# Layer 2's expert rows go to sorted places by indirect scatters instead of being fetched by inverted indices, and layer 1's experts run in a fixed VectorE order

## The chip, the cores and the metric

The kernel runs on one core of a Trainium2 chip, as one program in one launch. The metric is the device time of that program in microseconds (us), from its first instruction to its last, as a median of several runs. The engines are called as in the profile: PE is TensorE (matmuls and transposes), DVE is VectorE, ACT is ScalarE, POOL is GpSimd, and SP is SyncE, which issues DMA transfers. POOL issues the indirect DMAs, in which a column of indices says which row of a DRAM table each of 128 partitions reads or writes. A tile is 128 rows (tokens) of 128 floats.

## The reference: what is computed

The input is 2 x 1024 tokens of 128 numbers. Four layers follow each other, each of the form half an FFN, attention, half an FFN, all on a residual stream x:

```
for layer in 0, 1, 2:
    x = x + 0.5 * ffn(layernorm(x));  x = x + attn(layernorm(x));  x = x + 0.5 * ffn(layernorm(x))
layer 3:  the same, with a recurrence in the place of attention
```

Two of the FFNs matter here.

Layer 1's FFN picks, for every token and each of 8 blocks j, one of 64 hidden units by an argmax, and uses that unit alone:

```
lr   = x @ m1                                   # 128 -> 64
quant_mask = argmax(lr @ m2 + mb, axis=-1)      # per token: 8 choices out of 64
mid  = relu(x @ w1)[j, quant_mask[j]]           # of 512 hidden units, 8 stay
out  = mid @ w2[j, quant_mask[j]] + b2
```

Layer 2's FFN is a mixture of 8 experts, of which each token uses two:

```
gate_vals, gate_idx = top_k(x @ router_w, 2);  gates = softmax(gate_vals)
h   = gelu(x @ w1[e] + b1[e])                   # 128 -> 512
res = x + h @ w2[e] + b2[e]
y   = sum over the two experts of gates * (normed(res) * gamma[e] + beta[e])
```

## The kernel before

**Tokens and order of work.** x stays in SBUF as 16 tiles of 128 tokens, in four quarters of four tiles. The order of PE's instructions is the order in which the program is written (`manual_schedule(engines={PE})`); instructions of the other engines are ordered by a list scheduler at build time, which goes by its own cost model, unless `keep_in_program_order` holds them in the written order. Side work is woven into PE's order by a virtual clock: `later` starts a thread of small pieces with pauses between them, `tick(us)` moves the clock on and lets the threads whose pause is over do their next piece, and `need` finishes a thread at once. PSUM is split into three kinds of buffers, two of each: `pair` (two banks), `long` and `bank` (one bank each).

**Layer 1's FFN** (`l1_ffn`, L700 to L774) runs twice: once ahead of layer 1's attention (914 to 1012 us of the profile) and once after it (1482 to 1590 us), where the norms, the router and the routes of layer 2 are woven in by ticks. For every tile t there are these steps:

- `choose`: two matmuls into the two banks of one pair, the mask logits (L717) and the hidden units (L718); DVE takes the maximum of every block, mx (L722), and marks where it is, eq (L723); POOL multiplies eq by descending numbers, so that the first of equal maxima is largest (L724); ACT takes the relu of the hidden units, av (L726).
- `first`: DVE takes the maximum of the multiplied marks, fi (L732), and POOL subtracts it (L733), so that the chosen unit stands at zero.
- `chosen`: DVE multiplies av by "eq is zero" (L736).
- `output`: PE transposes av (L741), ACT copies it to aT (L743). `add`: PE multiplies by w2 (L748, L750), DVE adds the product to x (L751).

In iteration t stand first(t-1), chosen(t-2), choose(t), output(t-4) and add(t-5), with ticks of 5.0 us of virtual time in all.

**Layer 2's experts.** The tokens are taken in two halves of 1024, twice: e1 is the FFN ahead of layer 2's attention, e2 the one after it. A half goes through these steps:

- `l2_ffn_prep` normalizes two quarters, stores the normalized rows to a DRAM table xd (L1253, by SP) and computes router and gates.
- `l2_route` finds for every (token, choice) pair its place in a list sorted by expert, in which each expert's rows start at a new tile: counts by PE (L1290 to L1296), then small DVE operations that end in r_si, the 16 columns of places (L1321), and r_exi, the expert of each tile (L1326). At most 23 tiles can be in use. Then the places are inverted: DVE makes one-hot matrices (L1330 to L1342), PE multiplies them (L1347, 16 matmuls), and DVE turns the product into r_tok (L1354, L1355), which says for every place which token stands there.
- `L2Experts` works on the 23 tiles in groups of four. `gather` (L1396) fetches each tile's rows from xd by r_tok, with one indirect DMA on POOL per tile. `fetch` (L1409) loads the tile's expert weights, w1b and b2g, with SP. `ahead` keeps two or three groups of rows and six tiles of weights ahead. Then PE transposes the rows (L1442), computes the hidden layer (L1454) and the output (L1470), and DVE and SP normalize and store the result to a DRAM table yd.
- `l2_back` (L1539) fetches every token's two results from yd by r_si, with indirect DMAs on POOL, and adds them to x.

Of the kernel before, what the change touches and what calls it, by code (L numbers as in the profile page):

```python
# [19 lines left out]
P = 128  # L20
# [161 lines left out]

def norm_pieces(c, r, q, scale=1.0, eps=1e-5, weight=None, by=2, wait=(4.5, 4.0)):


    def xs(j):
        return c.x[:, 4 * q + j, :]

    def apply():
        r["xn"] = c.act.tile([P, 4, P], F32, tag="xn", name="xn", bufs=2)  # L190
        norm_apply(c, r, xs, r["xn"], 0, by)

    def turn():
        r["xT"] = by_feature(c, q if by == 2 else 0, r["xn"], weight)

    return [partial(norm_stats, c, r, xs, (scale, eps)), wait[0], apply, wait[1], turn, 2.0]
# [503 lines left out]
def l1_ffn(c, w, rs, key, done, ticks=1):  # L700
    nc = c.nc
    with c.pool("l1f", 2) as pool:
# [11 lines left out]
        def choose(t):  # L714
            s_ = slice(t % 4 * P, (t % 4 + 1) * P)
            pr = c.pair("pr")
            nc.tensor.matmul(pr[:, 0, :], lhsT=rs[t // 4]["lr"][:, s_], rhs=w["m2mb"], start=True, stop=True)  # L717
            nc.tensor.matmul(pr[:, 1, :], lhsT=rs[t // 4]["xT"][:, s_], rhs=w["w1"], start=True, stop=True)  # L718
            pm = pr[:, 0, :].rearrange("p (j y) -> p j y", j=8)
            mx = pool.tile([P, 8], F32, tag="mx", name="mx")  # L720
            eq = pool.tile([P, 8, 64], F32, tag="eq", name="eq", bufs=4)
            nc.vector.tensor_reduce(mx, pm, AX.X, ALU.max)  # L722
            nc.vector.tensor_tensor(eq, pm, mx.unsqueeze(2).to_broadcast([P, 8, 64]), ALU.is_equal)  # L723
            nc.gpsimd.tensor_mul(eq, eq, w["rev"].unsqueeze(1).to_broadcast([P, 8, 64]))  # L724
            av = pool.tile([P, 512], F32, tag="av", name="av", bufs=5)
            nc.scalar.activation(av, pr[:, 1, :], AF.Relu)  # L726
            return eq, av

        def first(eq, av):

            fi = pool.tile([P, 8], F32, tag="fi", name="fi")
            nc.vector.tensor_reduce(fi, eq, AX.X, ALU.max)  # L732
            nc.gpsimd.tensor_sub(eq, eq, fi.unsqueeze(2).to_broadcast([P, 8, 64]))  # L733

        def chosen(eq, av):
            nc.vector.scalar_tensor_tensor(av, eq.rearrange("p j y -> p (j y)"), 0.0, av, ALU.is_equal, ALU.mult)  # L736

# [18 lines left out]
        av, aT = {}, {}  # L756
        for t in range(NT + 5):
            if 0 <= t - 1 < NT:
                first(*av[t - 1])
            if 0 <= t - 2 < NT:  # L760
                chosen(*av[t - 2])
            if t < NT:
                av[t] = choose(t)
                if t % 4 == 2 and t // 4 < 3:
                    latent(t // 4 + 1)
            if ticks > 1:
                c.tick(5.0 / ticks)
            if 0 <= t - 4 < NT:
                aT[t - 4] = output(t - 4, av.pop(t - 4)[1])
            if ticks > 2:  # L770
                c.tick(5.0 / ticks)
            if 0 <= t - 5 < NT:
                add(t - 5, aT.pop(t - 5))
            c.tick(5.0 / ticks)  # L774

# [409 lines left out]
def l2_consts(c, pool):  # L1185
    w = {n: c.load(pool, f"l2f_{n}") for n in "router beta".split()}

    nc = c.nc
    shapes = dict(iota=[P], lower=[8, 8], pidx=[1], tcol=[2, 8])
    w |= {n: pool.tile([P] + shape, F32, tag=n, name=n) for n, shape in shapes.items()}  # L1190
    w["before"] = pool.tile([P, P], BF16, tag="before", name="before")
    nc.vector.tensor_scalar(w["before"], c.causal, -1.0, None, ALU.is_lt)
    pi = c.bank("pi")
    nc.tensor.matmul(pi[:, 0:P], lhsT=c.ones16, rhs=w["before"], start=True, stop=True)
    nc.tensor.matmul(pi[:, P : P + 1], lhsT=w["before"], rhs=c.ones16[:, 0:1], start=True, stop=True)
    nc.vector.tensor_copy(w["iota"], pi[:, 0:P])
    nc.vector.tensor_copy(w["pidx"], pi[:, P : P + 1])
    for k in range(2):
        nc.vector.tensor_copy(w["tcol"][:, k, :], pi[:, 0:8])
    eight = w["iota"][:, 0:8]  # L1200
    nc.vector.tensor_tensor(
        w["lower"],
        eight.unsqueeze(2).to_broadcast([P, 8, 8]),
        eight.unsqueeze(1).to_broadcast([P, 8, 8]),
        ALU.is_gt,
    )
    return w
# [22 lines left out]


def l2_half(c, dpool, name, qs):


    h = {"name": name, "qs": qs, "ready": 0, "then": []}
    h["xd"] = dpool.tile([S, P], F32, tag=f"xd{name}", name="xd")
    h["yd"] = dpool.tile([TILES * P, P + 1], F32, tag=f"yd{name}", name="yd")
    return h


def l2_ffn_prep(c, w, keep, h, a):
    nc = c.nc
    q, r = h["qs"][a], {}
    tiles = slice(4 * a, 4 * a + 4)
    norm = norm_pieces(c, r, q, by=8)

# [4 lines left out]

    def store():
        nc.sync.dma_start(out=h["xd"][512 * a : 512 * a + 512, :].rearrange("(j p) d -> p j d", p=P), in_=r["xn"])  # L1253

    def chosen():
        h["ready"] += 1
        if h["ready"] == 2:
            c.later(("route", h["name"]), l2_route(c, w, keep, h) + h["then"])
# [4 lines left out]
    )  # L1263
    return [begin] + norm[:3] + [store] + norm[3:] + gates[:1] + [chosen] + gates[1:]


def l2_route(c, w, keep, h):
# [59 lines left out]

    def one_hot():
        hi, hif, lo = tile_([16], "hi", I32), tile_([16], "hif"), tile_([16], "lo")
        nc.vector.tensor_scalar(hi, h["si"], 7, None, ALU.logical_shift_right)  # L1330
        nc.vector.tensor_copy(hif, hi)
        nc.vector.scalar_tensor_tensor(lo, hif, -float(P), r["sl"], ALU.mult, ALU.add)
        b = tile_([16, 24], "b")
        r["b"] = tile_([16, 2, 24], "b16", BF16)
        nc.vector.tensor_tensor(b, wide(w["iota"][:, 0:24], 16), long(hif, 24), ALU.is_equal)
        nc.vector.tensor_scalar(r["b"][:, :, 0, :], b, w["pidx"], None, ALU.mult)
        nc.vector.tensor_tensor(r["b"][:, :, 1, :], b, long(w["tcol"].rearrange("p k t -> p (k t)"), 24), ALU.mult)
        r["lo"] = lo

    def one_hot_row():  # L1340
        r["a"] = tile_([16, P], "a", BF16)
        nc.vector.tensor_tensor(r["a"], wide(w["iota"], 16), long(r["lo"], P), ALU.is_equal)  # L1342

    def invert():
        pt = r["pt"] = c.bank("pt")[:, 0:48]
        for k in range(16):
            nc.tensor.matmul(  # L1347
                pt, lhsT=r["a"][:, k, :], rhs=r["b"][:, k].rearrange("p a i -> p (a i)"), start=(k == 0), stop=(k == 15)
            )

    def tokens():
        h["tok"] = keep.tile([P, 24], I32, tag="r_tok", name="r_tok", bufs=2)
        low = tile_([24], "low")
        nc.vector.tensor_copy(low, r["pt"][:, 0:24])  # L1354
        nc.vector.scalar_tensor_tensor(h["tok"], r["pt"][:, 24:48], float(P), low, ALU.mult, ALU.add)  # L1355

    return [pairs, 2.0, count, 1.0, places, one_hot, one_hot_row, 9.0, invert, 1.0, tokens, 0.1]


class L2Experts:  # L1360
# [12 lines left out]
    def routed(self, n):  # L1373

        h = self.groups[n][0]
        return "tok" in h

# [11 lines left out]
    def gather(self):  # L1389
# [3 lines left out]
        self.xg[n] = self.keep.tile([P, 4, P], F32, tag="xg", name="xg", bufs=4)  # L1393
        for j, i in enumerate(g):
            at = bass.IndirectOffsetOnAxis(ap=h["tok"][:, i : i + 1], axis=0)
            self.nc.gpsimd.indirect_dma_start(self.xg[n][:, j, :], None, h["xd"], at)  # L1396
        self.gathered += 1
# [20 lines left out]
    def ahead(self, k):  # L1418

        h = self.groups[self.tiles[k][0]][0]  # L1420
        if "tok" not in h:
            for a in range(2):
                self.c.need(("half", h["qs"][a]))
            self.c.need(("route", h["name"]))

        some = 2 if any(self.c.waits(("back", h["name"])) for h in self.halves) else 3
        while self.gathered < min(self.tiles[k][0] + some, len(self.groups)) and self.routed(self.gathered):
            self.gather()
# [612 lines left out]
def macaron(ctx: ExitStack, tc: tile.TileContext, dram: dict, out: bass.AP):  # L2041
# [36 lines left out]
    with ExitStack() as s1:  # L2078
        with tc.tile_pool(name="w0", bufs=1) as p0:
            w = l0_weights(c, p0)  # L2080
            sets = l2_sets(c, dpool)
            r = [chunks() for _ in range(8)]
            for q in range(NC):
# [20 lines left out]
        wa = l2_attn_weights(c, s2.enter_context(c.pool("w2a")))  # L2104
        def halves(n, parts):

            hs = [l2_half(c, dpool, f"{n}{k}", qs) for k, qs in enumerate(parts)]

# [3 lines left out]

            return hs, prep

        h1, prep1 = halves(1, ((0, 1), (2, 3)))
        h2, prep2 = halves(2, ((0, 2), (1, 3)))
        s4 = ctx.enter_context(ExitStack())
# [145 lines left out]
```

## Time and profile before

| | |
|---|---|
| median of 7 runs | 2940.45 us (2939.42 to 2948.44) |
| the profiled execution's own time | 2940.06 us |
| its span, first to last instruction | 2938.3 us, so 1.76 us lie outside the span |
| mean granted TensorE clock | 0.952 of full speed |
| busiest engine | PE, 89% of the span |

The table of the profile's instructions names engine, line and operation, as in "DVE L732 ... fi<-eq": VectorE, line 732, writes fi from eq. In the timeline a row gives start, length, and, in brackets, how long the engine had stood idle before it and which instruction on which engine ended that. The lengths of neighbours can overlap a little, as an instruction's start is logged before its predecessor's end. A row "x4" stands for four instructions of one kind in a run. The windows give busy time per engine in a stretch of the span:

| window (us) | PE busy | DVE busy | ACT busy | POOL busy | granted clock |
|---|---|---|---|---|---|
| 920 to 960 | 34.82 | 32.64 | 12.18 | 22.30 | 0.91 |
| 960 to 1000 | 30.59 | 35.32 | 14.83 | 22.25 | 0.87 |
| 1520 to 1540 | 10.74 | 14.73 | 5.06 | 6.93 | 0.75 |
| 1540 to 1560 | 15.89 | 18.21 | 5.40 | 8.23 | 0.91 |
| 1560 to 1580 | 12.77 | 12.73 | 4.71 | 3.35 | 0.68 |
| 1580 to 1600 | 13.73 | 11.78 | 6.31 | 10.84 | 0.84 |

Indirect DMAs on POOL take 0.95 us of its time each and follow each other every 1.25 us. There are 92 of them for xg (`gather`; the median from issue to landing is 3.4 us) and 64 for yg (`l2_back`; 3.1 us).

### The profile page before, as it was taken

How to read it: one execution, taken by the hardware profiler on the slowest of the kernel's cores; microseconds unless marked ns; L12 is line 12 of the kernel's file. 1: busy time of each engine (PE TensorE's matmuls, PEld its weight loads, DVE VectorE, ACT ScalarE, POOL GpSimd, SP SyncE). 2: the span in 40 equal slices, each digit the busy share in tenths (PEclk: the TensorE clock that was granted, in tenths of full speed). 3: DMA queues.
4: the chain of work that ended last, by engine and by line, in shares of the span. 5: the costliest groups of instructions: out<-in, count | busy, mean ns of one | idle time of the engine just before them, and what ended most of it. 6: DMA issues, size and time to landing. Idle time of an engine off the chain costs nothing. (4 is left out here: it accounts for less than half of the span.)

```text
span 2938.3 us, 42431 instructions
## 1 busy us (share of the span) xinstructions
PE 2606.5 (89%) x14226; PEld 1492.1 (51%) x14226; DVE 2061.0 (70%) x6460; ACT 1597.2 (54%) x3188; POOL 1011.9 (34%) x941
## 2 busy tenths in 40 slices
PE   8899999899999779988977859999989999879999
PEld 5544445444465555444446843333433433776667
DVE  5566667666656888869666667777876776668874
ACT  3355555455533456666623517667766777444543
POOL 0133322223203554445433444334443443442110
PEclk9899999999999878999998979999999999889999
DMA  4000000000000000000002820000000011650000
GB/s 126 8 15 15 15 15 8 15 15 8 8 22 1 1 1 1 1 1 1 30 33 84 227 60 2 1 1 1 1 1 8 1 38 43 174 157 22 1 5 11
DMA packets 69768, 86.52 MB, mean 29 GB/s; under 512 B 14334, under 2 KB 49935, under 8 KB 68912
## 3 DMA queue, kind: packets, MB, share of 16 engines
q1 hardware_dynamic: 60816, 71.71, 8.7%
q0 software_dynamic: 4992, 10.27, 1.7%
q8 instruction: 114, 1.87, 0.3%
q10 hardware_dynamic: 3744, 1.84, 0.2%
q14 instruction: 102, 0.84, 0.1%
HBM read 66.18 MB, written 12.38 MB: 27 GB/s over the span
## 5 line engine op out<-in xcount | busy, mean ns | idle before, releaser
L1694 ACT ACTIVATE pe<-ps 128x1024 f32<-128x1024 f32 x256 | 249.1, 1021 | 205.5 <-PE ps L1687 205.5
L518 ACT ACTIVATE pe<-ps,nm 128x512 f32<-128x512 f32 (+3 forms) x384 | 219.8, 578 | 144.6 <-DVE nm L516 121.6
L1687 PE MATMUL ps<-tr 64*128 64x512 f32 x1024 | 262.6, 632 | 0.0
L1720 PE MATMUL po<-pe,v 128*64 128x512 f32 x1024 | 250.9, 611 | 1.0 <-ACT pe L1695 1.0
L1695 ACT ACTIVATE pe<-pe 128x2048 f32<-128x2048 f32 x128 | 244.6, 1911 | 4.0
L516 DVE TENSOR_REDUCE nm<-ps 128x2 f32<-128x256 f32 (+1 forms) x192 | 183.1, 954 | 60.8 <-PE ps L505 56.8
L348 DVE SCALAR_TENSOR_TENSOR x<-py,gates,x 128x128 f32<-128x128 f32 x448 | 133.1, 343 | 130.4 <-PE py L311 130.4
L505 PE MATMUL ps<-kT,qT 64*128 64x512 f32 (+3 forms) x768 | 179.4, 545 | 16.2 <-ACT pe L518 9.2
L533 PE MATMUL ptp<-ident,pe 128*128 128x128 f32 x1152 | 172.6, 284 | 16.0 <-ACT pT L104 9.4
L533 PEld LDWEIGHTS ptp<-ident,pe 128*128 128x128 f32 x1152 | 123.8, 141 | 116.5 <-issue 56.2
L547 PE MATMUL po<-pT,v 128*64 128x512 f32 (+3 forms) x768 | 166.7, 513 | 0.0
L1463 ACT ACTIVATE hT<-ph,w1b 128x128 f32<-128x128 f32 x368 | 105.4, 368 | 98.9 <-issue 62.2
L1707 POOL TENSOR_TENSOR acp<-pe 128x1024 f32<-128x1024 f32 x32 | 78.3, 2446 | 219.9 <-ACT pe L1695 196.5
L1720 PEld LDWEIGHTS po<-pe,v 128*64 128x64 f32 x1024 | 62.8, 138 | 174.5 <-issue 159.7
L104 ACT COPY pT<-ptp 128x512 f32<-128x512 f32 x192 | 91.9, 478 | 108.3 <-PE ptp L533 107.5
L1072 POOL TENSOR_SCALAR pe<-pe,rs 128x256 f32<-128x256 f32 (+7 forms) x128 | 95.2, 757 | 139.8 <-DVE rs L1069 56.6
L1687 PEld LDWEIGHTS ps<-tr 64*128 64x128 f32 x1024 | 90.4, 190 | 103.9 <-issue 72.6
L311 PEld LDWEIGHTS py<-l3f_w,hT 128*128 128x128 f32 x1024 | 126.8, 197 | 23.4 <-issue 19.1
L1610 POOL TENSOR_TENSOR sq<-raw 128x512 f32<-128x512 f32 x64 | 88.6, 1385 | 138.1 <-DVE raw L1608 104.0
L468 POOL TENSOR_TENSOR kT<-tab 128x512 f32<-128x512 f32 x32 | 40.6, 1268 | 266.8 <-DVE tab L467 135.7
L311 PE MATMUL py<-l3f_w,hT 128*128 128x128 f32 x1024 | 128.8, 281 | 2.5 <-ACT hT L300 2.5
L1454 PE MATMUL ph<-xgT,w1b 128*128 128x128 f32 x736 | 109.8, 297 | 21.8 <-ACT hT L1463 11.6
(418 smaller groups left out, 6264.4 us busy)
## 6 DMA issues: line engine op xcount, KB each, us to landing
w1b<-sets SPq DMA_DIRECT2D x92, 258.0 KB
b2g<-sets SPq DMA_DIRECT2D x92, 128.0 KB
two<-two SPq DMA_DIRECT2D x64, 128.0 KB
yd<-y SPq DMA_DIRECT2D x20, 258.0 KB
l2f_w<-in_l2f_w SPq DMA_DIRECT2D x2, 2048.0 KB
sets<-in_l2f_w SPq DMA_DIRECT2D x1, 2048.0 KB
xd<-xn SPq DMA_DIRECT2D x8, 256.0 KB
l3f_w<-in_l3f_w SPq DMA_DIRECT2D x2, 1024.0 KB
```

Source lines behind the costliest of these rows:

```text
L311: nc.tensor.matmul(py[:, j, :], lhsT=hT[:, k, j * P : (j + 1) * P], rhs=w2[:, e, k, :], start=(k == 0), stop=(k == hc - 1),)
L348: c.nc.vector.scalar_tensor_tensor(x, py[:, j, :], rs[q]["g"][:, j, e : e + 1], x, ALU.mult, ALU.add)
L505: nc.tensor.matmul(ps[:, h, :W], lhsT=u["qT"][r, q0 : q0 + P], rhs=u["kT"][r, gk * 512 : gk * 512 + W], start=True, stop=True,)
L516: nc.vector.tensor_reduce(nm, ps[:, :, :W], AX.X, ALU.max, negate=True)
L518: nc.scalar.activation(u["pe", n][:, h, i, :W], ps[:, h, :W], AF.Exp, bias=nm[:, h : h + 1], accum_out=u["rs"][:, n, i, h : h + 1],)
L533: nc.tensor.transpose(pt[:, i * P : (i + 1) * P], u["pe", n][:, h, i, j * P : (j + 1) * P], c.ident)
L547: nc.tensor.matmul(u["po", n][r, lo * P :], lhsT=u["v"][:, BLOCKS[n][1] * 4 + j, cols], rhs=u["pT", n, j][h][:, lo * P :], start=(j == 0), ...
L1454: nc.tensor.matmul(ph[:, a * P : (a + 1) * P], lhsT=t[:, a * P : (a + 1) * P], rhs=xT[n][:, j * P : (j + 1) * P], start=True, stop=True,)
L1687: nc.tensor.matmul(ps[:, h, :], lhsT=tr[r, 1, p, k * P : (k + 1) * P], rhs=tr[r, 0, p, q * 512 : (q + 1) * 512], start=True, stop=True,)
L1694: nc.scalar.activation(pe[:, j], ps, AF.Tanh, scale=1.0 / 50.0)
L1695: nc.scalar.activation(pe, pe, AF.Exp, scale=50.0 * 0.125)
L1720: nc.tensor.matmul(u["po"][r, :], lhsT=u["v"][:, k, 2 * u["p"] + h, :], rhs=pe[:, j, h, :], start=(k == 0), stop=(k == TB - 1),)
```

## The change

Two things are changed.

In `l1_ffn` the relu's matmul gets a bank of its own (pa) where it was the second half of the pair. An iteration now does the matmuls, mx and the relu of tile t first, then first(t-1), chosen(t-2) and at last eq(t), and three of the DVE operations (fi, av and eq) are held in the written order. The built order of VectorE is mx(t), fi(t-1), av(t-2), eq(t). The ticks come to 4.4 us instead of 5.0.

In layer 2's experts the inversion is gone: no one-hot matrices, no 16 matmuls, no r_tok, no table xd and no stores to it, and two constants less. The normalized rows of a half stay in SBUF (tag hx). A DRAM table xs of 23 x 128 rows per half takes them in sorted order: 16 indirect DMAs on POOL per half write every token's row to its two places by r_si (64 in all). xs is filled with zeros once, at the start of the program, by four DMAs of SP of 1.5 MB each. `gather` is one plain DMA of SP per group (24 in all), which reads four tiles of xs in order and waits for all 16 scatters of its half. The scatters wait for the zeros and are declared independent of each other. Groups are always fetched three ahead.

The core of the diff:

```diff
 def choose(t):
-    pr = c.pair("pr")
-    nc.tensor.matmul(pr[:, 0, :], lhsT=rs[t // 4]["lr"][:, s_], rhs=w["m2mb"], start=True, stop=True)
-    nc.tensor.matmul(pr[:, 1, :], lhsT=rs[t // 4]["xT"][:, s_], rhs=w["w1"], start=True, stop=True)
+    pr, pa = c.pair("pr")[:, 0, :], c.bank("pa")
+    nc.tensor.matmul(pr, lhsT=rs[t // 4]["lr"][:, s_], rhs=w["m2mb"], start=True, stop=True)
+    nc.tensor.matmul(pa, lhsT=rs[t // 4]["xT"][:, s_], rhs=w["w1"], start=True, stop=True)
...
+def equal(pm, mx, av):
+    pin(nc.vector.tensor_tensor(eq, pm, mx.unsqueeze(2).to_broadcast([P, 8, 64]), ALU.is_equal))
+    nc.gpsimd.tensor_mul(eq, eq, w["rev"].unsqueeze(1).to_broadcast([P, 8, 64]))
...
 for t in range(NT + 5):
+    new = choose(t) if t < NT else None
     if 0 <= t - 1 < NT:
         first(*av[t - 1])
     if 0 <= t - 2 < NT:
         chosen(*av[t - 2])
     if t < NT:
-        av[t] = choose(t)
+        av[t] = equal(*new)
...
 def l2_half(c, dpool, name, qs):
-    h["xd"] = dpool.tile([S, P], F32, tag=f"xd{name}", name="xd")
+    h["xs"] = dpool.tile([TILES * P, P], F32, tag=f"xs{name}", name="xs")
+    h["zeros"] = c.nc.sync.dma_start(
+        out=h["xs"].rearrange("(i p) d -> p i d", p=P), in_=c.zeros.unsqueeze(1).to_broadcast([P, TILES, P])
+    )
...
 def l2_route(c, w, keep, h):
-    return [pairs, 2.0, count, 1.0, places, one_hot, one_hot_row, 9.0, invert, 1.0, tokens, 0.1]
+    def scatter(a, k):
+        for j in range(4):
+            at = bass.IndirectOffsetOnAxis(ap=h["si"][:, TB * k + 4 * a + j :][:, 0:1], axis=0)
+            row = nc.gpsimd.indirect_dma_start(h["xs"], at, h["xn"][a][:, j, :], None)
+            c.tc.declare_no_dep(row.ins, group=h["name"], reason="no two rows share a place")
+            c.tc.add_to_no_dep_group(h["name"], row.ins)
+            after(c, row, h["zeros"])
+            h["rows"].append(row)
+    rows = [x for a in range(2) for k in range(2) for x in (partial(scatter, a, k), 3.0)]
+    return [pairs, 2.0, count, 1.0, places, 5.0] + rows
...
 def gather(self):
-    for j, i in enumerate(g):
-        at = bass.IndirectOffsetOnAxis(ap=h["tok"][:, i : i + 1], axis=0)
-        self.nc.gpsimd.indirect_dma_start(self.xg[n][:, j, :], None, h["xd"], at)
+    rows = h["xs"][g[0] * P : (g[0] + len(g)) * P, :].rearrange("(j p) d -> p j d", p=P)
+    load = self.nc.sync.dma_start(out=self.xg[n][:, 0 : len(g), :], in_=rows)
+    for row in h["rows"]:
+        after(self.c, load, row)
```

`after` adds a wait of one DMA for another. `routed`, which says whether a half's rows and weights may be fetched, now asks for r_si and a finished route thread, where it asked for r_tok.

## The prediction

> **What bounds the kernel now.** I read the page's engine shares first, then the chain of waits and the timelines of the three places the change touches: layer 1's half-FFN (914 to 1012 us, and 1482 to 1590 us, where layer 2's router and routes are woven in), the start of the first experts (e1, 1575 to 1595 us), and of the second (e2, 2484 to 2513 us). Shares of the span:
>
> ```profile
> PE 2606.5 (89%) x14226; PEld 1492.1 (51%) x14226; DVE 2061.0 (70%) x6460; ACT 1597.2 (54%) x3188; POOL 1011.9 (34%) x941
> ```
>
> TensorE (PE) carries the span, so time changes only where PE stands still. In layer 1's half-FFN it does, for a loop between VectorE (DVE) and GpSimd (POOL). First the DVE timeline of one tile, then POOL's (start, length, instruction; in brackets the idle time before it and who ended it):
>
> ```profile
> 944.17 0.69 DVE L732 TENSOR_REDUCE fi<-eq 128x8 f32<-128x512 f32 x1 [0.67 <-POOL eq L724]
> 944.78 0.68 DVE L722 TENSOR_REDUCE mx<-pr 128x8 f32<-128x512 f32 x1
> 946.08 0.69 DVE L736 SCALAR_TENSOR_TENSOR av<-eq,av 128x512 f32<-128x512 f32 x1 [0.63 <-POOL eq L733]
> 946.69 0.68 DVE L723 TENSOR_TENSOR eq<-pr,mx 128x512 f32<-128x512 f32 x1
> 948.75 0.69 DVE L732 TENSOR_REDUCE fi<-eq 128x8 f32<-128x512 f32 x1 [0.85 <-POOL eq L724]
> ```
>
> ```profile
> 942.87 1.27 POOL L724 TENSOR_TENSOR eq<-eq,l1c_rev 128x512 f32<-128x512 f32 x1 [1.41 <-DVE eq L723]
> 945.00 1.04 POOL L733 TENSOR_TENSOR eq<-eq,fi 128x512 f32<-128x512 f32 x1 [0.29 <-DVE fi L732]
> 947.46 1.27 POOL L724 TENSOR_TENSOR eq<-eq,l1c_rev 128x512 f32<-128x512 f32 x1 [1.41 <-DVE eq L723]
> ```
>
> The reader sees a ring: fi, POOL's subtraction, av (which waits for that same subtraction), eq, POOL's multiplication, next fi: 948.75 - 944.17 = 4.58 us. Over four tiles eq advances from 934.10 to 951.21, 4.28 per tile. PE alone, where not held, takes 3.40 (this product starts at 939.42, 942.82, 946.23). At e1 the PE timeline shows the count matmul, the last token transposes and the first hidden matmul:
>
> ```profile
> 1574.92 0.24 PE L1290 MATMUL pc<-r_m,before 128*128 128x64 bf16 x1 [4.75 <-DVE r_m L1283]
> ...
> 1594.13 0.33 PE L1442 MATMUL pt<-ident,xg 128*128 128x128 f32 x1 [0.58 <-DMA xg<-xd,r_tok]
> 1595.19 1.22 PE L1454 MATMUL ph<-xgT,w1b 128*128 128x128 f32 x4 [0.73 <-ACT xgT L104]
> ```
>
> DVE has the places (r_si) at 1579.68 and the inverse (r_tok) at 1585.51; POOL then issues a gather per tile:
>
> ```profile
> 1585.81 1.17 POOL L1396 DMA_INDIRECT xg<-xd,r_tok  x1 [13.09 <-DVE ln_rs L120]
> 1587.28 0.95 POOL L1396 DMA_INDIRECT xg<-xd,r_tok  x1 [0.30 <-issue]
> ```
>
> That is 1.25 us per indirect DMA, and about 4.5 us from a gather's start to its transpose (4.49, 4.69, 4.35). At e2, attention's tail lies beside the same steps:
>
> ```profile
> 2498.68 0.58 PE L1347 MATMUL pt<-r_b,r_a 128*128 128x48 bf16 x16 [4.27 <-DVE r_b L1337]
> ...
> 2508.55 3.35 PE L1664 MATMUL py<-l2a_wo,aoT 128*128 128x128 f32 x14 [4.45 <-DVE aoT L1736]
> 2511.70 1.06 PE L1442 MATMUL pt<-ident,xg 128*128 128x128 f32 x4
> 2513.44 0.82 PE L1454 MATMUL ph<-xgT,w1b 128*128 128x128 f32 x5 [0.68 <-ACT xgT L104]
> ```
>
> The transposes don't wait for the gather here (issued from 2502.46): it hid behind attention.
>
> **Part A and B: layer 1's loop.** The fixed order is mx(t), fi(t-1), av(t-2), eq(t): av no longer waits for the subtraction of its own round. fi at 0; subtraction at 0.83 (944.17 to 945.00), 1.42 long when av runs beside it (row at 1497.34 us) against 1.04 alone, so done at 2.25; multiplication 1.27, done at 3.52; fi again at 3.55. DVE's own sum, .69+.68+.69+.68+.28+.28 = 3.3, and PE's 3.40 fit under it. ScalarE's relu gets a PSUM bank of its own and no longer waits for eq (35.3 us of such waits from 1475 to 1590); that unlocks PE's waits on it (.3 to 1.3 each), which the same 3.55 already covers.
> A, first run: about eight tiles run at the ring's pace; 8 x 0.8 = 6.4, taken as -7. In the rest (960 to 1000) DVE is busy 35.32 of 40 us and gives nothing. Bounds: -12 (all 16 tiles) and 0.
> B, second run: eq(8) would come at 1514.6 and not 1520.8, -6. Behind it the norm of quarter 0 (21 small DVE operations from 1520.78 to 1534.23, PE waiting 8.41 us for its xn) and the router set the pace; the wait stays, and the remaining tiles give 3 more. B = -9, count at 1566. Bounds: -15 (every tile at the new pace) and -3 (half of the -6).
>
> **Part C: start of e1.** The one-hot tables (DVE, about 4.6 us), 16 inverse matmuls (0.57) and the r_tok step go: from r_si to the first gather now 6.1 us. In their place 16 scatters, all of which must land before the first plain load. From r_si: 0.3 to the first, 15 x 1.25 = 18.75 to the start of the last, 3.9 to its landing (between the median 3.4 of the gathers' landings and the 4.5 above), 0.4 SP issue, 3.2 until 256 KB are usable (w1b, 258 KB: 1637.32 to 1640.07 = 2.75; 1643.33 to 1647.09 = 3.76): 26.6. Then four transposes on a slow clock 1.0 and 0.7 to the hidden matmul: 28.3. Before: 1595.19 - 1579.68 = 15.5. C = +12.8. PE has only the last four tiles of layer 1 to cover it (some 9 us). Bounds: +8 (2.4 landing, 2.75 load, and a clock that stays up) and +16 (5.2 landing, as the slowest gathers of yd, and 3.76).
>
> [...] No row of before shows a scatter. [...]
>
> **Part D: middle of e1.** SP issues in order. The seventh group's load stands before set 22's weights and waits for half 1's scatters. Half 1's count came at H0 + 22 (H0, the first hidden matmul, 1595.19; count 1617.30), and with it now two tiles later H0 + 26; + 3.5 to the places + 23 = H0 + 52.5. Set 22 follows and is usable 3 to 6 us later, needed at H0 + 56.2 (1651.39). D = +1, bounds 0 and +3.
>
> **Part E: start of e2.** r_si ends 2492.41 (a 3.34 reciprocal lies in its chain, and stays); + 26.6 = 2519.0, + 1.7 = 2520.7 against 2513.44. E = +7.3. PE's 4.27 wait goes with the inverse, but the transposes wait for the scatters, so it is swallowed. Bounds +4 and +11, from the same ends.
>
> **Part F: middle of e2.** PE's order is unchanged but for the inverse. Count of half 1 at 2533.67; the blocked load goes at count + 26.2, set 19 behind it at + 27.4, usable at + 30.2 to 31.2; its hidden matmul came at 2561.27 = count + 27.6. PE stands 3.1 us and pays 1.4 of slow clock after it (a stall of 8.41 before 1534.78 was followed by some 5 us of pairs at 1.91 instead of 1.02). F = +4.5, bounds 0 and +8.
>
> **What costs nothing.** 92 gathers leave POOL (115 us) and 64 scatters come (80 us): POOL is 34% busy. In e1's tail PE stood 4.91 + 1.00 + 2.58 us for xg queued behind 16 yg gathers; the next transposes, at 1698.89, then waited 1.07 more for an xn that hangs on those same yg, so the wait only changes its name: 0, bounds -8 and 0. Zero filling is 6 MB by SP at the start, behind the copies of the sets; the rates there are 128 to 310 GB/s until 40 us and near zero until 117.86, when the next DMAs are issued, so at 128 it takes 47 us and is done by 90; its cover is that pause, and gone it would cost 0 to 5. The eight stores of xd go, and two constants: hidden. pa takes turns with the transposes in the two single PSUM banks; ScalarE, which empties both, is busy 12.18 of 40 us: 0, and at worst 0.3 per tile (the least of PE's waits on it now), +10 over 32 tiles.
>
> **Sum:** -7 - 9 + 12.8 + 1 + 7.3 + 4.5 = +9.6 on the profiled execution's 2940.06 (0.39 under the median): 2949.7, given as 2950. A measurement of this kernel tells about 0.2%, 5.9 us, from no change: this is slower.
>
> **The rivals.**
> Faster: the ring opens for most tiles (A -10, B -13) and the round trip is short (C +8, E +5, F +2): -8, 2932. It decides where A and B together pass the cost of the scatters; for: the ring is nearly clean in 16 of 32 tiles, and PE is never over 90% busy there; against: DVE at 88% in the second half of the first run.
> Even: A -10, B -12 against 23 of scatters, +1: 2941.
> Worse: the gain of the ring is lost where DVE and POOL hold each other up. At 938.01 an av took 1.74 beside a multiplication begun at 937.93. If the subtraction starts before av, av ends it: fi 0, subtraction .83 to 1.87, av to 2.5, eq, multiplication to 4.56: 4.58 again, A = -1, B = -3: 2962. It decides by 0.2 us: av can start 0.60 after fi, the subtraction 0.83. [...]
> Not what it says: if the build left DVE's order as it was, only B's relu would gain; the order of the built kernel shows mx, fi, av, eq, so I leave it out.
>
> **How the numbers follow.** Forecast (2946 to 2957) 0.40; worse (to 2968) 0.18; even 0.18; faster 0.22; beyond, above all a longer block of SP, 0.02. Slower by over 0.2% is 0.60, within 0.17, faster 0.23, the edges moved by one point. The range leaves about a tenth below and less above: from the middle of the faster case, 2931, to 2965. The forecast alone, from its terms' bounds taken half each, is 2940 to 2957.
>
> **What would show it.** Right: fi to fi of 3.5 us in 939 to 955; the count of half 0 some 16 us earlier; 16 scatters 1.25 apart, the first transpose of e1 26 to 27 us behind r_si with PE idle before it; a PE wait on w1b near the twentieth tile of e2. Wrong: av of 1.7 in each tile (worse); a scatter landing under 2.5 or over 5 us; layer 1's tiles still being done when the scatters land, so that C vanishes.

## The result, and the profile after

The changed kernel takes 2956.33 us (median of 17 runs) beside 2942.92 us of the kernel before (42 runs): a ratio of 1.0043, 95% interval 1.0034 to 1.0051, so 13 us slower. The profiled execution has a span of 2952.2 us, 13.9 us more than before.

The engine shares in the page of the changed kernel:

```profile
PE 2620.1 (89%) x14161; PEld 1504.4 (51%) x14161; DVE 2036.1 (69%) x6421; ACT 1596.2 (54%) x3188; POOL 995.3 (34%) x914
```

DVE and POOL have 25 and 17 us less to do, and PE's busy time is 14 us longer, though it has fewer instructions. Layer 1's ring, first DVE's timeline and then POOL's:

```profile
940.74 0.69 DVE L738 TENSOR_REDUCE fi<-eq 128x8 f32<-128x512 f32 x1 [0.25 <-POOL eq L732]
941.34 0.68 DVE L742 SCALAR_TENSOR_TENSOR av<-eq,av 128x512 f32<-128x512 f32 x1
941.94 0.68 DVE L731 TENSOR_TENSOR eq<-pr,mx 128x512 f32<-128x512 f32 x1
...
943.07 0.67 DVE L724 TENSOR_REDUCE mx<-pr 128x8 f32<-128x512 f32 x1
944.19 0.69 DVE L738 TENSOR_REDUCE fi<-eq 128x8 f32<-128x512 f32 x1 [0.45 <-POOL eq L732]
```

```profile
944.95 1.42 POOL L739 TENSOR_TENSOR eq<-eq,fi 128x512 f32<-128x512 f32 x1 [0.80 <-DVE fi L738]
946.33 1.26 POOL L732 TENSOR_TENSOR eq<-eq,l1c_rev 128x512 f32<-128x512 f32 x1
```

Here fi comes after 3.45 us (944.19 - 940.74), where it was 4.58 and 3.55 was forecast. Four of the 15 steps of this run are that short; towards its end they take 5 to 7 us, as DVE then has other work too. The last fi comes 9.6 us earlier than before (984.94, before 994.54). The subtraction takes 1.42 beside av, and av 0.68. The start of the first experts, in PE's timeline:

```profile
1570.60 0.23 PE L1302 MATMUL pc<-r_m,before 128*128 128x64 bf16 x1 [4.46 <-DVE r_m L1295]
...
1600.10 1.09 PE L1436 MATMUL pt<-ident,xg 128*128 128x128 f32 x4 [19.67 <-DMA xg<-xs]
1601.92 1.44 PE L1448 MATMUL ph<-xgT,w1b 128*128 128x128 f32 x5 [0.73 <-ACT xgT L104]
```

The count is 4.3 us earlier than before, and the first hidden matmul 6.7 us later; in between PE stands 19.67 us for the loads. POOL's last scatter of this half, and SP's first load of its rows:

```profile
1594.76 0.97 POOL L1344 DMA_INDIRECT xs<-xn,r_si  x1 [0.30 <-issue]
```

```profile
1597.15 1.49 SPq L1390 DMA_DIRECT2D xg<-xs  x3
```

So the load goes out 2.4 us after the start of the last scatter. Landings that the trace records for scatters within the trains take 2.2 to 5.0 us, 3.5 in the median (16 of the 64 are recorded). At the start of the second experts PE waits 11.11 us for the same loads, and in both middles 3 us for a set of weights (PE's timeline):

```profile
1659.60 2.08 PE L1448 MATMUL ph<-xgT,w1b 128*128 128x128 f32 x8 [3.48 <-DMA w1b<-sets]
...
2522.92 1.08 PE L1436 MATMUL pt<-ident,xg 128*128 128x128 f32 x4 [11.11 <-DMA xg<-xs]
2524.68 2.08 PE L1448 MATMUL ph<-xgT,w1b 128*128 128x128 f32 x8 [0.68 <-ACT xgT L104]
...
2577.15 1.78 PE L1448 MATMUL ph<-xgT,w1b 128*128 128x128 f32 x8 [3.06 <-DMA w1b<-sets]
```

The span in stages, each between the same two instructions of the two profiles:

| stage | before | after | difference | forecast |
|---|---|---|---|---|
| layer 0 | 912.57 | 912.95 | +0.4 | 0 |
| layer 1's FFN, first run | 100.74 | 99.23 | -1.5 | A: -7 |
| layer 1's attention | 468.53 | 472.78 | +4.2 | 0 |
| FFN, second run, to the count of half 0 | 93.08 | 85.64 | -7.4 | B: -9 |
| count to first hidden matmul, e1 | 20.27 | 31.32 | +11.0 | C: +12.8 |
| e1, first hidden to last | 135.70 | 132.82 | -2.9 | D: +1 |
| layer 2's attention, to the next count | 753.36 | 753.41 | +0.1 | 0 |
| count to first hidden matmul, e2 | 29.19 | 36.53 | +7.3 | E: +7.3 |
| e2, first hidden to last | 126.60 | 132.22 | +5.6 | F: +4.5 |
| layer 3 | 298.25 | 295.27 | -3.0 | 0 |

Two lines ask for a reason: A, where the ring opened as forecast and nothing came of it, and layer 3, in which nothing was changed.

### The profile page after: what moved, and what is told of

It is laid out like the page before. It is cut to its first block, busy times and chain, and to the rows that moved or that the text cites. A ratio compares the mean times of both kernels' runs of the same rounds, so it can differ in the third digit from the quotient of the medians.

```text
span 2952.2 us, 42233 instructions
## 1 busy us (share of the span) xinstructions
PE 2620.1 (89%) x14161; PEld 1504.4 (51%) x14161; DVE 2036.1 (69%) x6421; ACT 1596.2 (54%) x3188; POOL 995.3 (34%) x914
## 5 line engine op out<-in xcount | busy, mean ns | idle before, releaser
L1681 PEld LDWEIGHTS ps<-tr 64*128 64x128 f32 x1024 | 90.6, 191 | 103.7 <-issue 72.2
L314 PEld LDWEIGHTS py<-l3f_w,hT 128*128 128x128 f32 x1024 | 125.0, 195 | 23.9 <-issue 19.7
L1448 PE MATMUL ph<-xgT,w1b 128*128 128x128 f32 x736 | 112.1, 301 | 27.8 <-ACT hT L1457 12.6
```

The source lines that it names most:

```text
L314: nc.tensor.matmul(py[:, j, :], lhsT=hT[:, k, j * P : (j + 1) * P], rhs=w2[:, e, k, :], start=(k == 0), stop=(k == hc - 1),)
L1448: nc.tensor.matmul(ph[:, a * P : (a + 1) * P], lhsT=t[:, a * P : (a + 1) * P], rhs=xT[n][:, j * P : (j + 1) * P], start=True, stop=True,)
L1681: nc.tensor.matmul(ps[:, h, :], lhsT=tr[r, 1, p, k * P : (k + 1) * P], rhs=tr[r, 0, p, q * 512 : (q + 1) * 512], start=True, stop=True,)
```

## The experiments

**The chips.** The experiments ran on two other chips, on which the kernel before itself takes 3030 to 3032 us, where it took 2942.92 for the result above; "the first chip" is the place of that result and of the first two profiles. The second chip ran most of the kernels below, the third the new loop in the first run alone, the dense matmuls, the late load and the last version. The kernel before has no profile there, but in the versions that keep its stages those up to the first experts have the same lengths (the old loop's first run takes 100.8 to 101.1 us); the 90 us lie in the experts, e1 and e2, and some in layer 3. Whether the chips themselves differ, or something else between the sessions, is not on record. Ratios below are against runs of the kernel before on the same chip, 25 to 35 of them in each group; stages are compared within these two chips.

**One part alone.** Layer 1's function of the changed kernel was put into the kernel before, and the other way round.

```diff
 # new loop, old experts                  # new experts, old loop
-l1_ffn of before                        -l1_ffn of after
+l1_ffn of after                         +l1_ffn of before
```

> Layer 1's new loop in both runs, layer 2's experts as before (gathers by inverted indices). The profile of the changed kernel shows the ring at 3.45 us per tile in both runs, and yet the first run ended only 1.5 us earlier, with 34 us at half clock in it where there were 17. Theory (the ring's gain is real, and in the first run it is lost to the clock and to VectorE's later work): the count of half 0 comes 5 to 8 us earlier than before, the first experts start as much earlier, total 3 to 8 us faster (0.1 to 0.3%). Rival 1 (the loss in the first run was the chance of one execution): A and B come in full, 14 to 18 us faster. Rival 2 (the loop brings nothing over the whole): within 2 us of before.

> Layer 2's scatters and plain loads, layer 1's loop as before. Theory (each of the two starts pays 11 and 7 us for 16 scatters in series, and each middle 3 us of wait on a weight set behind a blocked load): 17 to 24 us slower than before. Rival (the scatters cost little and the new loop of layer 1 is what made the changed kernel slower): under 8 us slower.

Measured: the loop alone 0.9975 (0.9964 to 0.9986), 7.5 us faster; the experts alone 1.0014 (1.0002 to 1.0027), 4 us slower, far less than the 17 to 24 expected. As the experts' stages on these chips are so much longer, the changed kernel was run here as a control, with the experts alone once more.

> The changed kernel itself, as the control beside which the other three of this group are read. Between the chip of the first profiles and the one of the group before, the experts' stages differ by some 30 to 40 us each (first hidden matmul to last: 136 and 127 us there, 165 to 172 here), so differences are taken within one chip. Theory (the cost of the scatters is hidden in part where the experts' loads are slow): 0.4% slower than before on a chip like the first, about level with before on a chip like the second.

> Layer 2's scatters with layer 1's loop as before, on this chip. Theory (parts add up): slower than the changed kernel by what layer 1's loop gains alone, 6 to 9 us. Rival (the loop gives nothing once the scatters follow it): within 3 us of the changed kernel.

Measured: the changed kernel 0.9992 (0.9979 to 1.0004), level with before here; the experts alone 1.0007 (0.9995 to 1.0020). The parts add up: 0.9975 and 1.0007 to 1.0014 make 0.998 to 0.999. The experts alone are also 4 to 5 us slower than the control, which is the same gain once more. So the loop is worth 5 to 8 us here. The scatters cost 0.7 to 1.4 thousandths, 2 to 4 us, where the four stages of the experts on the first chip sum to 21 us (11.0 - 2.9 + 7.3 + 5.6); the experts alone were not run there.

**Which run of the loop gains.**

```diff
-l1_ffn(c, w1, r[3], "d", follow("e", prep))     # first run: the old loop
+l1_ffn_old(c, w1, r[3], "d", follow("e", prep))
 l1_ffn(c, w1, r[5], "f", prep1, 3)              # second run: the new loop
```

> Layer 1's new loop in its second run alone; the first run's loop and layer 2's experts as before. Theory (the first run's gain is lost, on the clock or behind it): 5 to 9 us faster than before, and not slower than the kernel with the new loop in both runs. Rival (the first run gains too): 3 us or more slower than the kernel with the new loop in both runs.

> Layer 1's new loop in its first run alone, all else as before. In the profiles so far the first run is 4 to 5 us shorter with the new loop, and layer 1's attention behind it 3 to 5 us longer, with 95 to 105 us at half clock in it where the old loop left 85 to 92. Theory (the gain of the first run is given back in the attention, at half clock): within 2 us of before. Rival (it was chance, and the step of the prediction holds): 4 to 8 us faster.

Measured: the new loop in the second run alone 0.9973 (0.9959 to 0.9987), 8.2 us faster, as much as the loop in both runs. In its profile, however, the second run's stage up to the count takes 89.9 us, only 3 less than the 92.9 to 93.1 of the old loop; the other profiles with the new loop there have 85.6 to 90.0, and the more of it lies at half clock (24 to 39 us), the longer it is. Where the rest of the 8.2 us comes from was not found. In the first run alone it is worth 0.9992 (0.9978 to 1.0007), nothing that can be told from no change. The windows of the new loop in the first run, then of the old one on the same chip (the first line is the FFN's first run, the second layer 1's attention; the last three numbers are PE's granted clock, DMA share and GB/s):

```profile
912.00:1008.00 96.00, 86.13 (x332) 46.63 (x331) 83.99 (x208) 36.24 (x71) 59.19 (x65) 0.87 0.00 1
1008.00:1482.00 474.00, 416.20 (x2413) 238.22 (x2412) 357.28 (x1705) 282.29 (x788) 222.00 (x310) 0.90 0.02 6
```

```profile
918.00:1019.00 101.00, 84.42 (x342) 45.92 (x341) 87.84 (x214) 36.58 (x73) 56.11 (x67) 0.92 0.00 1
1019.00:1487.00 468.00, 410.70 (x2398) 233.53 (x2396) 353.86 (x1699) 280.84 (x786) 222.18 (x308) 0.91 0.01 5
```

The new loop's run is 5 us shorter, at a clock of 0.87 and not 0.92, and the attention behind it 5 us longer, at 0.90 and not 0.91. In time at half clock the attention has 98.2 us and not 88.7. A matmul of 512 columns takes 1.91 us at half clock and 1.02 at full (before, L717 at 1535.81 and 1542.13); by an estimate from these, ten us more at half clock are some five us lost, which is the size of the loss. It is PE's busy time that grew, by 5.5 us (416.20 - 410.70); its idle time is the same (57.8 and 57.3). The other profiles, on all three chips, agree. In the eight with the new loop in the first run this run takes 92.9 to 99.2 us and the attention 472.8 to 477.2, with 95 to 105 us of it at half clock. In the six with the old loop it is 100.7 to 101.1 and 468.5 to 472.2, with 75 to 92 us. The sum of the two stages is the same: 566.7 to 573.4 and 569.2 to 573.1. The profiles of the first chip show where it begins (windows before, then after):

```profile
980.00:1012.00 32.00, 26.70 (x114) 15.31 (x114) 28.57 (x77) 16.29 (x35) 21.35 (x37) 0.84 0.00 1
1012.00:1060.00 48.00, 37.19 (x213) 31.73 (x213) 37.39 (x169) 21.77 (x75) 18.62 (x33) 0.63 0.00 1
```

```profile
980.00:1012.00 32.00, 32.00 (x95) 18.04 (x95) 21.13 (x59) 12.52 (x26) 18.28 (x35) 0.57 0.00 1
1012.00:1060.00 48.00, 39.77 (x213) 34.87 (x212) 36.72 (x168) 21.88 (x75) 15.67 (x31) 0.56 0.00 1
```

From 980 to 1012 us PE is busy throughout in the changed kernel, 32.00 of 32, and does fewer matmuls than before (95 and not 114), at a clock of 0.57. The time DVE saved was spent by PE at half clock. The long spell at half clock at the attention's start lasts 44.4 us in all eight profiles with the new loop, and 34.1 in four of the six with the old.

**What the clock follows.** In layer 1's attention PE stands at half clock for 34 us (1017.9 to 1052.0 before) without an idle gap over 2 us, in matmuls of 6 to 192 columns.

```diff
 gates():   # behind the gate matmuls of the second quarter
+    pw = c.long("pw")
+    for k in range(4):
+        nc.tensor.matmul(pw, lhsT=w["w1"][:, 0:P], rhs=w["w1"], start=True, stop=True)
```

> The kernel before with four dense matmuls added (128x128 by 128x512, results unused) behind the second quarter's gate matmuls, at the start of layer 1's attention, where PE is never idle for more than 2 us and yet runs at half clock for 34 us (1017.9 to 1052.0). They cost 4 us at full clock and 7.6 at half. Theory (the clock follows how much work the matmuls carry, and these many matmuls of 6 and 128 columns keep it low although PE is busy): the spell ends 15 to 20 us earlier, the total moves by -6 to +2 us. Rival (the clock follows idle gaps alone): the spell keeps its end relative to the work and the total is 4 to 8 us slower.

Measured: 1.0009 (0.9996 to 1.0021). The dense matmuls stand from 1035.98 to 1041.8, behind the second quarter's gate matmuls alone, and the windows show the spell end among them, at 1040.4, while before it went on to 1052 (before, then with the dense matmuls):

```profile
1018.00:1052.00 34.00, 26.98 (x142) 23.95 (x141) 24.65 (x112) 12.14 (x45) 9.59 (x18) 0.50 0.00 1
```

```profile
1020.00:1040.00 20.00, 16.55 (x62) 13.49 (x63) 12.28 (x44) 4.08 (x8) 3.85 (x8) 0.50 0.00 0
1040.00:1064.00 24.00, 19.32 (x112) 14.17 (x110) 18.97 (x110) 14.41 (x63) 10.68 (x18) 0.64 0.00 1
```

The spell is 20.5 us long and not 34.1, as expected if the clock follows the work that matmuls carry and not idle gaps alone. The next spell then came sooner (1047.2 to 1064.2, where before it was 1058.8 to 1062.2), so that the two together are as long as they were, 37.6 us and 37.5. Over the whole attention 75 us lie at half clock and not 85, and it still takes 469.2 us, within the 468.5 to 472.2 of the other profiles with the old loop. So the half clock was moved by dense work, in this one profile, and nothing was won by it.

**What a start costs.** Only 8 of a half's 16 scatters are issued.

```diff
-rows = [x for a in range(2) for k in range(2) for x in (partial(scatter, a, k), 3.0)]
+rows = [x for a in range(2) for k in range(1) for x in (partial(scatter, a, k), 3.0)]
```

> The changed kernel with 8 scatters per half instead of 16: the rows of each token's second choice are left out, and their places hold zeros; every load, matmul and gather stays. Theory (a start is 0.3 us, then scatters one after another at 1.26 us, 2.4 us to the last landing, 3.1 us of load): from the places to the first transpose 16 us instead of 26 in e1 and e2, both middles' waits on w1b shorter or gone, total 18 to 26 us faster than the changed kernel. Rival 1 (one fixed latency of the round trip through DRAM sets the start, not the number of scatters): under 8 us. Rival 2 (the starts are covered by other late work): the first transposes move by 10 us, the total by less than half of it.

Measured: from the places to the first transpose 15.3 us in e1 and 15.8 in e2, where the control on this chip has 25.4 and 25.9. That is the 10 us that eight scatters at 1.27 us make, and rivals 1 and 2 fall. The wait for the loads in PE's timeline of e1:

```profile
1590.29 1.09 PE L1436 MATMUL pt<-ident,xg 128*128 128x128 f32 x4 [8.81 <-DMA xg<-xs]
```

The total is 0.9860 (0.9841 to 0.9880), 42 us under the control, more than the 18 to 26 expected. Twenty of it are the two starts. The other 22 lie in the middles (e1 151.3 us and not 163.0, e2 147.9 and not 158.4), so on this chip a scatter costs something there too. (Half the rows stay away in this kernel, so it shows times only.)

**Who holds the weights in the middles.** Two ways to keep SP's queue free of the load that waits for half 1's scatters: loads issued on POOL, and the first of them asked for later.

```diff
-load = self.nc.sync.dma_start(out=self.xg[n][:, 0 : len(g), :], in_=rows)
+load = self.nc.gpsimd.dma_start(out=self.xg[n][:, 0 : len(g), :], in_=rows)
```

```diff
 while self.gathered < min(self.tiles[k][0] + 3, len(self.groups)) and self.routed(self.gathered):
+    if self.gathered == len(GROUPS) and self.tiles[k][0] + 1 < len(GROUPS):
+        break
     self.gather()
```

> The changed kernel with the group loads issued on POOL instead of SP, so that SP's queue of weight loads is not held by a load that waits for half 1's scatters. Theory (the waits of 3.48 and 3.06 us on w1b in the middles of e1 and e2 come from that hold): both waits vanish, the middle of e2 is 3 to 5 us shorter, total 3 to 7 us faster than the changed kernel. Rival (the sets are late for another reason, the load of the DMA queues): the waits on w1b stay and the total is within 2 us of the changed kernel, or slower by the POOL time of 24 loads of about 1.3 us each.

> Group loads issued on POOL, against the changed kernel on the same chip. Theory (SP's queue of weights is held by the load that waits for half 1's scatters, 3.48 us in e1 and 3.06 us in e2): 3 to 7 us faster than the changed kernel, and the two waits on w1b in the middles are gone. Rival: within 2 us of it.

> The changed kernel with the first group of half 1 loaded one group ahead instead of three, so that SP reaches that load only when half 1's scatters are about to land. Theory (SP's queue of weight loads is held by that load): the waits on w1b in the middles go, 3 to 6 us faster than the changed kernel on a chip with the first profiles' load rates, 0 to 3 us where the loads themselves are the bound. Rival (nothing is held): within 1 us on either.

Measured: loads on POOL 0.9970 (0.9958 to 0.9981) and, beside the control of 0.9992, 0.9987 (0.9975 to 1.0000): the same as the control. The later load: 1.0004 (0.9994 to 1.0013), on the third chip, where the changed kernel itself was not run. (The 1.3 us per load of the rival is near the 1.27 at which the scatters follow each other.) Neither helps clearly, and in these profiles the middles wait for something else. In the control PE stands 16.49 us at one hidden matmul of e1:

```profile
1657.80 1.44 PE L1448 MATMUL ph<-xgT,w1b 128*128 128x128 f32 x5 [16.49 <-ACT hT L1457]
```

ACT, which reads its bias from the same set of weights, stands 11.66 us just before, with no releaser shown, and DVE 12.60. It looks as if a set of weights came late. SP's queue with the later load, in which no load of rows stands, shows a hole of 12.6 us, but DVE stood first: here its wait ends at 1646.53, and SP's next load goes out 0.4 us after DVE's y begins. SP's rows, then DVE's:

```profile
1637.22 0.07 SPq L1405 DMA_DIRECT2D w1b<-sets  x1
1649.85 0.33 SPq L1405 DMA_DIRECT2D b2g<-sets  x1
```

```profile
1646.53 0.69 DVE L1485 TENSOR_TENSOR res<-py,xg 128x512 f32<-128x512 f32 x1 [12.62 <-remote]
1649.47 1.14 DVE L1494 SCALAR_TENSOR_TENSOR y<-res,mean,b2g 128x128 f32<-128x128 f32 x4
```

POOL's scatters of half 1 run from 1632.99 to 1653.2 there. The DMA queues from 1642 to 1650 us, in the changed kernel on the first chip, then on the second (q1 carries the plain transfers, q0 POOL's indirect ones):

```profile
q1 hardware_dynamic: 1259, 1.22, 58.4%
q0 software_dynamic: 190, 0.39, 14.5%
```

```profile
q0 software_dynamic: 201, 0.40, 14.5%
```

While the scatters run, the first chip moves 1.22 MB of plain transfers beside them in 8 us, and the second none at all. That alone would read as if the burst stopped the loads, but nothing was left to move: in the control SP had issued 45 plain transfers from 1572 to 1642 us, 9.41 MB, and the queue moved 9.42 MB in that time. So the sets asked for had been moved, the empty queue and SP's hole are consequences of the standstill, and what began it, on PE, ACT and DVE at once, does not stand in the traces. That it falls within the scatters shows no more than that both stand at one time. The same holds for the 16 yg gathers: in the kernel with the new loop in the first run alone, whose experts are those of before, PE stands 23.48 us while these and the xg gathers queued after them run, and there plain loads do go on (1.80 MB from 1686 to 1702 us). That the scatters have a part in it is shown by the run with half of them, whose middles are 10 to 12 us shorter.

The total is level on these chips because the starts cost 17.2 us (31.2 and 35.6 us from count to hidden matmul, beside 20.4 and 29.2 with gathers on the third chip), and the stages from first to last hidden matmul give 19.7 back (163.0 and 158.4 beside 170.9 and 170.2 there). Beside the new loop in the second run alone, on the same chip as the control, it is 15.5 and 14.6. That the middles gain because no xg gathers stand behind those of yg any more would fit, but was not tested. Why the chips differ was not found; whether either version mends the 3 us waits of the first chip stays open, since none of them ran on it.

**A version from the findings.** New loop in the second run, half 0 by gathers as before, half 1 by scatters, its first load late.

```diff
+h["sorted"] = name[-1] == "1"       # half 1 of each stage: xs, scatters, plain loads
+                                    # half 0: xd, inverted places, gathers, as before
```

> What the experiments point to: layer 1's new loop in its second run alone; half 0 of each expert stage by gathers and inverted indices as before (its route stands on the path that starts the experts), half 1 by scatters and plain loads (its route lies beside half 0's experts), the first of its groups loaded one group ahead. Theory (the scatters cost time only where the experts wait for them): 8 us faster than before from layer 1 and 2 to 7 more from half 1, where no gathers stand behind those of the results on POOL: 0.3 to 0.5% faster than before. Rival (half 1's scatters cost as much as they save): as the new loop in the second run alone, 0.27% faster.

Measured: 1.0007 (0.9995 to 1.0019). It loses what the loop alone wins. In e1 one wait of 15.0 us falls in the train of half 1's scatters, and another of 15.1 in that of the yg gathers, as in the control; at the start of e2 it stands 7.14 us at the first hidden matmul, for which no cause was found. The version to keep is the new loop in the second run alone, 0.27% faster than before on the second chip, the only one it ran on.

## Why the prediction was right, and where it was wrong

- **The ring** (3.55 forecast, 3.45 measured) held where nothing else held DVE up, in four steps of the first run and five of the second, with the subtraction at 1.42 and av at 0.68. The rival in which DVE and POOL hold each other up needed av at 1.7 in each tile and falls: one av of 16 took over 1.5 (1.53, at 986.27).
- **A failed** in its step "taken as -7": it took time saved in the first run for time saved in the kernel. The run did get shorter (1.5 us on the first chip, up to 8 on the others), but PE then works at half clock in its end and in the attention behind it (on the first chip 34.1 us of the run and not 17.1, and 95.6 us of the attention and not 85.3), and the two together are as long as before (+2.7 us here). The prediction weighed the clock only behind idle gaps; here it falls while PE is busy (32.00 of 32 us, at 0.57). That the half clock is the cause rests on its time, which fits the loss, on the 14 profiles, in which it goes with the loop of the first run, and on the run with dense matmuls, in which a spell ended among them; A itself was not run with the clock held.
- **B** was -7.4 for -9. Alone it timed at 8.2 us on the second chip, but only 3 of them lie in its stage there. The sign named for it failed: the count of half 0 came 4.3 us earlier and not some 16, as it carries A's loss and the attention's with it.
- **C and E** were +11.0 for +12.8 and +7.3 for +7.3, and half the scatters took off just the 10 us that the sum gave them. One term was mis-sized: landing and SP's issue, 3.9 and 0.4, took 2.4 from the start of the last scatter. By the prediction's own list a landing under 2.5 is a sign of being wrong; the sum held because other terms took part of it back. The scatters follow each other at 1.29 and 1.35 us on the mean, and start 0.9 and 0.3 behind the places. In e1 the places also stand 0.8 us nearer to the count than before, which the sum did not have. The 2.4 stand at the end of a train; the landings recorded within the trains, 3.5 in the median, are near the gathers' 3.4 that the 3.9 was taken from.
- **D** had the wrong sign. The wait for the weights came (3.48, forecast up to 3): SP issued nothing from 1648.69 to 1655.89 us, when half 1's first load went out, 2.39 behind the start of the last scatter, and sets followed from 1656.53. But the edit that was costed at nothing was not nothing: the waits for xg behind the yg gathers (8.49) went, and the wait for xn that follows grew from 1.07 only to 5.62, since xn was there 2.4 us sooner, counted from the first hidden matmul (101.3 and not 103.7), though the yg gathers start 2.4 later. Why it came sooner was not found. That is 3.9 us won, within the bounds of -8 and 0 and not at the end that was taken. The stage also had less half clock, 19.8 us and not 30.2.
- **F** was +5.6 for +4.5: the wait on weights came at 3.06 (3.1 forecast). The half clock grew from 23.9 to 32.3 us, but not where it was forecast: of the 8.4 more lie most at the stage's start, behind the 11.11 us wait, and 3.4 behind the wait on weights.
- **Layer 3's -3.0** was in no term. Nothing in it was changed. It spent 10.2 us at half clock before and 6.8 after, which makes at most 1.7 of the 3; the rest was not found. In the profiles of the other chips the same stage takes 304.6 to 308.5 us, so the sum above cannot be read finer than a few us.
- The total, +13.4 by the medians for +9.6, was right in sign and size by some luck: the miss of A (some 10 us with the attention) was partly met by D and layer 3. On the second chip "slower" would have been wrong, with 0.9992: there the middles win back what the starts cost, and no row of the one profile shows that.

## What to carry to other kernels

The time that the new loop saved in the first run was not saved in the kernel, as PE's clock did not hold (on the third chip 5 us less in the run, 5 more in the attention, with 98.2 us at half clock there and not 88.7): compare the granted clock of the stage and of the one behind it, not only the stage's length. Indirect DMAs on POOL came one after another at 1.27 us here, and the last of 16 started 19.3 us behind the first, so put a train of them where nothing waits for the last. When a queue moves nothing, count what was issued into it before calling it blocked: here it was empty, with 9.41 MB issued and 9.42 moved. Where a data movement is the change, measure it on more than one chip: this one was 1.0043 on the first and 0.9992 on the second.

## What the hardware showed that was not expected

- PE's clock has two levels in the traces, 1.0 and 0.5, and its spells at half last whole multiples of 3.4 us (10.2 and 34.1 before, 44.4 after, 20.5 with the dense matmuls). They come also where PE is never idle for more than 2 us, with matmuls of 6 to 192 columns and transposes (1017.9 to 1052.0 us before). PE was busy for 32.00 of 32 us by the profile at a clock of 0.57 (980 to 1012 us after), so being busy there was not enough to keep the clock up.
- On the two chips of the experiments PE stands still for 10 to 23 us at a time in the middles, where its longest wait there in the two profiles of the first chip is 7.25 us. The waits of e1 fall within trains of indirect DMAs. In 8 us of one no plain transfer moves (0 MB, beside 1.22 MB on the first chip), but all that SP had issued was already there. As nothing waited in the plain queue, these rows do not show whether one kind of transfer holds up the other.
